# Windowed attention laid out by even and odd heads on the query partitions, with attention times values on eight array tiles

## The chip, the cores and the metric

One core of a Trainium2 chip, everything in fp32. The metric is the time of one execution on the device, in microseconds, median over several runs. The kernel before takes 4977.4 us (median of 3 runs, 4976.43 to 4993.0). PE is the matrix engine (TensorE), DVE the vector, ACT the scalar and POOL the GpSimd engine. A "row" is one row of eight 7x7 windows of one image; there are 32 images x 8 = 256 rows.

## The reference, cut to what matters

```python
# x: (32, 56, 56, 128); window 7x7 (49 tokens), 4 heads of 32 channels, shift by 3
def window_attention(x):                       # layer 0, after a group norm
    xs  = roll(x, (-3, -3)); win = windows(xs) # (B*64, 49, 128)
    q, k, v = split(win @ w_qkv.T)             # (.., 4 heads, 49, 32)
    attn = q * 32**-0.5 @ k.T + relative_bias + shift_mask
    out  = softmax(attn) @ v
    return roll(unwindow(out @ w_proj.T + b_proj), (3, 3))
x = x + window_attention(gn(x))
# layer 1: cosine transforms, mixing of 32 modes, back, and a feed-forward 128-512-128
x = x + feedforward(fourier(gn(x)))
```

The program runs the attention of one image together with layer 1 of the image before, so that PE has other work while attention waits for the other engines.

## The kernel before: the parts that the change and the argument touch

```python
# one row of windows, i; WT = 49, JP = 64, HD = 32, RT = 392
def attn_scores(im, i):
    pq = attn_bank()                               # query projection, copied by ACT into q
    nc.tensor.matmul(pq[:, :RT], lhsT=im.w[:, 0:C], rhs=src, ...)
    nc.scalar.activation(q[:, :RT], pq[:, :RT], AF.Identity, bias=im.bias[:, 0:1], scale=QS)
    pk = attn_bank()                               # key projection, then four fills of k_bd
    nc.tensor.matmul(pk[:, :RT], lhsT=im.w[:, C : 2 * C], rhs=src, ...)
    for h in range(NH):
        hs = slice(h * HD, (h + 1) * HD)
        dst = k_bd[hs, :, h % 2]                   # block diagonal: each head its own columns
        if h % 2:
            nc.vector.tensor_scalar(dst, pk3[hs], im.bias[hs, 1:2], None, ALU.add)
        else:
            nc.scalar.activation(dst, pk3[hs], AF.Identity, bias=im.bias[hs, 1:2])
    for w in range(NWR):                           # V, each window twice, by head parity hh
        for hh in range(2):
            nc.tensor.matmul(pv[hh * JP : hh * JP + WT, w * JP : (w + 1) * JP],
                             lhsT=src[:, w * WT : (w + 1) * WT], rhs=wv[:, hh], ...)
    # two ACT copies into v_bd; what lies off the head's own block stays zero
    for w in range(NWR):                           # scores: window parity on the partitions
        for hp in range(2):                        # hp: heads 0,1 or heads 2,3
            nc.tensor.matmul(
                ps[hp][(w % 2) * JP : (w % 2 + 1) * JP, (w // 2) * 2 * WT : (w // 2 + 1) * 2 * WT],
                lhsT=q[cs, w * WT : w * WT + JP],
                rhs=k_bd[cs, w].rearrange("c h j -> c (h j)"), ...)   # moves 98 columns
    # ... softmax on DVE, POOL, ACT ...

def attn_out(im, i):
    for hf in range(2):
        # 4 transposes into a bank, one DVE copy into aT, then per window (the last is cut in two)
        nc.tensor.matmul(po3[hp * JP : (hp + 1) * JP, :, x0 : x0 + s1 - s0],
                         lhsT=v[:, w, hp].rearrange("j h d -> j (h d)"),   # 128 x 64, half zeros
                         rhs=aT[:, 2 * (w4 // 2) + hp, w % 2, 0:WT]..., ...)
    nc.scalar.activation(oT[...], po[:, :RT], AF.Identity, bias=im.bias[:, 2:3])
    # ... projection by wproj, residual, store ...
```

## Time and profile before

| | kernel before |
|---|---|
| median time, first 3 runs | 4977.4 us |
| PE busy | 4641.3 us, 93% |
| DVE, ACT, POOL busy | 2428.6, 2491.8, 1385.5 us |
| one row, inner part | 18.88 us |

How to read the rest: PE's busy share says that it is the bound, but not how long each matmul holds it, since their records overlap. For that I use the start times of single records. A *group* is a run of matmuls of the same tiles (so the two projections L286 and L291 are one group where they adjoin); its *in-group time* goes from its first start to its last; its *switch* goes from its last start to the first start of the next group, less any wait; *idle* is what the profile calls a wait of PE. In-group, switch and idle add up to a row's length. I count from the start of row 40 to that of row 232 of each trace and divide by these 192 rows.

### The profile page before, as it was taken

Reading aid. Unit: us, or ns where it says so; the run is one execution under the profiler, and the core shown is the slowest. Engines: PE = TensorE matmul, PEld = TensorE weight load, DVE = VectorE, ACT = ScalarE, POOL = GpSimd, SP = SyncE. Lnnn points to the kernel's source line nnn. Section 1 sums busy time; section 2 is a strip of 40 time slices with the busy share of each in tenths; the row PEclk is TensorE's granted clock in tenths of the full one; section 3 lists DMA queues with packets and bytes.
Section 4 is the critical chain, followed back from the end, with each engine's and each line's share of the span. In section 5 each row is a group of like instructions: output and inputs, shape, how many; then the busy total and the mean of one; then the engine's idle time right before and its main releaser. Section 6 shows DMA issues by size and latency. Waiting matters only on the chain.

```text
span 4980.0 us, 143896 instructions
## 1 busy us (share of the span) xinstructions
PE 4641.3 (93%) x64320; PEld 3587.0 (72%) x64320; DVE 2428.6 (49%) x4469; ACT 2491.8 (50%) x4705; POOL 1385.5 (28%) x1071
## 2 busy tenths in 40 slices
PE   4799999999999999999999999999999999999998
PEld 3677777777777777777777777777777777777776
DVE  3554445554554545445544455544455544555441
ACT  2445555555555455554555555455554555554553
POOL 2222222232222323222232222222223232222220
PEclk8799999999999999999999999999999999999999
DMA  3111222212222212222212222122222122222111
GB/s 79 39 51 43 60 58 57 65 45 49 58 58 59 65 38 52 60 58 59 58 38 60 57 56 65 45 49 57 57 61 64 41 50 60 58 61 60 35 46 51
DMA packets 533292, 271.74 MB, mean 55 GB/s; under 512 B 29360, under 2 KB 532289, under 8 KB 532417
## 3 DMA queue, kind: packets, MB, share of 16 engines
q1 hardware_dynamic: 521272, 257.03, 20.3%
q8 instruction: 504, 8.26, 0.7%
q10 hardware_dynamic: 11400, 5.51, 0.4%
q14 instruction: 116, 0.94, 0.1%
HBM read 159.66 MB, written 102.76 MB: 53 GB/s over the span
## 4 chain that ended last, share of the span: by engine, by line
PE 72%; DVE 10%; ACT 7%; POOL 5%; issue 3%; DMA 2%; ACTq 1%; SPq 0%; POOLq 0%; DVEq 0%
PE pc L619 14%; PE pc L602 11%; PE pa L324 6%; PE pa L379 6%; PE pc L526 5%; PE pa L304 5%; POOL a L346 5%; PE pa L400 5%; PE pc L555 5%; PE pa L286 4%; PE pa L291 3%; DVE mx L345 3%; PE pa L365 2%; ACT a L349 2%; PE pa L230 2%
## 5 line engine op out<-in xcount | busy, mean ns | idle before, releaser
L619 PE MATMUL pc<-wff,hid 128*112 128x128 f32 x7168 | 926.5, 283 | 0.7 <-ACT hid L610 0.6
L619 PEld LDWEIGHTS pc<-wff,hid 128*112 128x112 f32 x7168 | 840.8, 182 | 55.1 <-issue 14.6
L346 POOL TENSOR_TENSOR a<-a,mx 128x784 f32<-128x784 f32 x256 | 389.0, 1519 | 1700.2 <-DVE mx L345 1586.2
L610 ACT ACTIVATE hid<-pc,b1sb 128x448 f32<-128x448 f32 x896 | 568.3, 634 | 487.4 <-PE pc L602 446.9
L602 PE MATMUL pc<-xf,wff 128*128 128x448 f32 x1792 | 781.1, 553 | 0.8 <-DVE xf L582 0.8
L349 ACT ACTIVATE a<-a 128x784 f32<-128x784 f32 x256 | 223.5, 873 | 835.5 <-POOL a L346 835.5
L297 DVE TENSOR_SCALAR k_bd<-pa,bqkv 32x392 f32<-32x392 f32 x512 | 320.7, 626 | 619.8 <-ACT k_bd L299 613.7
L352 POOL TENSOR_TENSOR a<-a,rs 128x784 f32<-128x784 f32 x256 | 389.1, 1520 | 678.1 <-DVE rs L351 595.8
L596 POOL TENSOR_TENSOR res<-res,b2sb 112x512 f32<-112x512 f32 x224 | 284.8, 1271 | 859.2 <-DMA res<-scr 837.5
L337 DVE TENSOR_TENSOR a<-pa,bm 128x392 f32<-128x392 f32 x512 | 284.8, 567 | 408.2 <-PE pa L324 403.5
L379 PEld LDWEIGHTS pa<-aT,v 128*64 128x64 f32 x9216 | 328.9, 142 | 166.4 <-DVE aT L371 121.1
L371 DVE COPY aT<-pa 128x512 f32<-128x512 f32 x512 | 346.1, 676 | 200.2 <-PE pa L365 199.9
L408 DVE TENSOR_TENSOR xl<-pa,xl 112x384 f32<-112x384 f32 (+1 forms) x256 | 159.9, 625 | 579.6 <-PE pa L400 579.6
L350 DVE TENSOR_REDUCE sm<-a 128x16 f32<-128x784 f32 x256 | 248.3, 970 | 387.5 <-ACT a L349 387.5
L324 PE MATMUL pa<-k_bd,q 64*64 64x98 f32 x8192 | 420.8, 252 | 16.6 <-DVE k_bd L297 13.7
L324 PEld LDWEIGHTS pa<-k_bd,q 64*64 64x64 f32 x8192 | 327.4, 133 | 143.4 <-DVE k_bd L297 85.3
L379 PE MATMUL pa<-aT,v 128*64 128x49 f32 (+2 forms) x9216 | 386.8, 227 | 35.7 <-DVE aT L371 33.5
L602 PEld LDWEIGHTS pc<-xf,wff 128*128 128x128 f32 x1792 | 300.4, 190 | 164.5 <-issue 91.8
L304 PEld LDWEIGHTS pa<-wn,xw 128*49 128x49 f32 x8192 | 258.8, 125 | 161.6 <-issue 63.4
L242 POOL TENSOR_TENSOR xl<-xl,bproj 112x384 f32<-112x384 f32 (+1 forms) x256 | 285.2, 1136 | 237.8 <-PE pa L230 234.3
L365 PE MATMUL pa<-ident,a 128*128 128x128 f32 x2048 | 334.8, 287 | 1.1 <-POOL a L352 1.1
L313 ACT COPY v<-pa 49x512 f32<-49x512 f32 x512 | 293.3, 573 | 78.0 <-PE pa L304 72.4
(83 smaller groups left out, 6687.3 us busy)
## 6 DMA issues: line engine op xcount, KB each, us to landing
res<-scr SPq DMA_DIRECT2D x224, 224.0 KB
htok<-scr SPq DMA_DIRECT2D x256, 196.0 KB
out_dram<-res SPq DMA_DIRECT2D x192, 224.0 KB
scr<-xl SPq DMA_DIRECT2D x128, 224.0 KB
xl<-in_x_dram SPq DMA_DIRECT2D x32, 784.0 KB
xl<-in_x_dram SPq DMA_DIRECT2D x32, 672.0 KB
scr<-xl SPq DMA_DIRECT2D x128, 168.0 KB
out_dram<-res SPq DMA_DIRECT2D x32, 112.0 KB
```

The costliest lines, as they stand in the source:

```text
L297: nc.vector.tensor_scalar(dst, pk3[hs], im.bias[hs, 1:2], None, ALU.add)
L304: nc.tensor.matmul(pv[hh * JP : hh * JP + WT, w * JP : (w + 1) * JP], lhsT=src[:, w * WT : (w + 1) * WT], rhs=wv[:, hh], start=True, stop= ...
L324: nc.tensor.matmul(ps[hp][qs, (w // 2) * 2 * WT : (w // 2 + 1) * 2 * WT], lhsT=q[cs, w * WT : w * WT + JP], rhs=k_bd[cs, w].rearrange("c h ...
L346: nc.gpsimd.tensor_tensor(a3, a3, mx2.unsqueeze(2).to_broadcast([P, 2 * NR, WT]), ALU.subtract)
L349: nc.scalar.activation(a3, a3, AF.Exp)
L352: nc.gpsimd.tensor_tensor(a3, a3, rs2.unsqueeze(2).to_broadcast([P, 2 * NR, WT]), ALU.mult)
L365: nc.tensor.transpose(pt[:, m * P : (m + 1) * P], a[:, hp, pr].rearrange("p h j -> p (h j)"), ident,)
L371: nc.vector.tensor_copy(aT.rearrange("p m a j -> p (m a j)"), pt)
L379: nc.tensor.matmul(po3[hp * JP : (hp + 1) * JP, :, x0 : x0 + s1 - s0], lhsT=v[:, w, hp].rearrange("j h d -> j (h d)"), rhs=aT[:, 2 * (w4 / ...
L602: nc.tensor.matmul(ph[:, :GT], lhsT=wff1[:, f * P : (f + 1) * P], rhs=xf[:, 8 * g : 8 * g + 8].rearrange("p r w -> p (r w)"), start=True, ...
L610: nc.scalar.activation(hf, ph[:, :GT], AF.Relu, bias=b1sb[:, f : f + 1])
L619: nc.tensor.matmul(pf[:TC, c * C : (c + 1) * C], lhsT=hid[f][:, c * TC : (c + 1) * TC], rhs=wff2[:, f], start=(f == 0), stop=(f == NF - 1),)
```

## The change

The intent is that attention times values does not multiply the zeros of a block-diagonal V. The query partitions of a score tile now hold head parity (u) where they held window parity. So the transposed attention has, on its first 64 partitions, an even window, and on the others an odd one (in the kernel before an even and an odd head, which is why V had to be block-diagonal there). Values can take 49 rows and 32 columns for each window and head, on eight tiles of the array. V gets half as many matmuls, twice as wide, and one copy instead of two. The price lies in scores: each moves 49 columns instead of 98, and there are twice as many. Output comes in two banks, by parity of the window, and is brought into order by ACT (one piece) and DVE (three pieces).

```diff
         for w in range(NWR):
             for hp in range(2):
                 cs = slice(hp * JP, (hp + 1) * JP)
-                qs = slice((w % 2) * JP, (w % 2 + 1) * JP)
-                nc.tensor.matmul(
-                    ps[hp][qs, (w // 2) * 2 * WT : (w // 2 + 1) * 2 * WT],
-                    lhsT=q[cs, w * WT : w * WT + JP],
-                    rhs=k_bd[cs, w].rearrange("c h j -> c (h j)"),
...
+                for u in range(2):
+                    nc.tensor.matmul(
+                        ps[hp][u * JP : (u + 1) * JP, w * WT : (w + 1) * WT],
+                        lhsT=q[cs, w * WT : w * WT + JP],
+                        rhs=k_bd[cs, w, u],
...
         for w in range(NWR):
-            for hh in range(2):
-                nc.tensor.matmul(
-                    pv[hh * JP : hh * JP + WT, w * JP : (w + 1) * JP],
-                    lhsT=src[:, w * WT : (w + 1) * WT],
-                    rhs=wv[:, hh],
...
+            t0 = i * RT + w * WT
+            nc.tensor.matmul(
+                pv[w % 2 * JP : (w % 2 + 1) * JP, (w // 2) * C : (w // 2 + 1) * C],
+                lhsT=im.xw[:, t0 : t0 + JP],
+                rhs=im.w[:, 2 * C : 3 * C],
...
+        nc.scalar.copy(v.rearrange("j p c -> j (p c)"), pv)
...
-                    for hp in range(2):
                         nc.tensor.matmul(
-                            po3[hp * JP : (hp + 1) * JP, :, x0 : x0 + s1 - s0],
-                            lhsT=v[:, w, hp].rearrange("j h d -> j (h d)"),
...
+            for p2 in range(2):
+                pr = 2 * hf + p2
+                for h in range(NH):
+                    for u in range(2):
+                        ks = slice(u * JP, u * JP + WT)
+                        nc.tensor.matmul(
+                            po[u][h * HD : (h + 1) * HD, pr * WT : (pr + 1) * WT],
+                            lhsT=v[ks, pr, h * HD : (h + 1) * HD],
+                            rhs=aT[ks, 2 * p2 + h // 2, h % 2, 0:WT],
...
-        nc.scalar.activation(
-            oT[:, i % 2 * RT : (i % 2 + 1) * RT], po[:, :RT], AF.Identity, bias=im.bias[:, 2:3]
-        )
+        # for each bank u: the piece of u = 0 on ACT, the three of u = 1 on DVE
+                if u:
+                    nc.vector.tensor_scalar(d, f, im.bias[:, 2:3], None, ALU.add)
+                else:
+                    nc.scalar.activation(d, f, AF.Identity, bias=im.bias[:, 2:3])
```

Cut: the bias and mask tables in the new order, the buffers, and the address arithmetic of the output pieces (the comment line stands for it).

More of the change, by code (lines that the diff above doesn't have):

```diff
@@ L152, in swin_fourier_kernel @@
     nc.sync.dma_start(rpb[JP : JP + WT], rpb[0:WT])
-    mask_sb = const_load([P, 2, 3, WT], shift_mask.rearrange("r s p j -> p r s j"), "mask")
-    bm = const.tile([P, 2, 2, NWR // 2, 2, WT], F32, tag="bm", name="bm")
-    rpb_f = rpb.rearrange("p (t h) y x -> p t h (y x)", t=2)
-    for r in range(2):
-        for pr in range(NWR // 2):
-            for t in range(2):
-                nc.vector.tensor_tensor(
-                    bm[:, r, t, pr],
-                    rpb_f[:, t],
-                    mask_sb[:, r, 0 if pr < NWR // 2 - 1 else 2]
-                    .unsqueeze(1)
-                    .to_broadcast([P, 2, WT]),
-                    ALU.add,
-                )
+    mask_sb = const.tile([P, 2, 2, WT], F32, tag="mask", name="mask")
+    nc.vector.memset(mask_sb, 0.0)
+    for hh in range(2):
+        rows = slice(hh * JP, hh * JP + WT)
+        for k, src in enumerate((shift_mask[:, 0, 0:WT], shift_mask[:, 2, JP : JP + WT])):
+            nc.scalar.dma_start(mask_sb[rows, :, k], src.rearrange("r p j -> p r j"))
+    bm = const.tile([P, 2, 2, NWR, WT], F32, tag="bm", name="bm")
+    nc.gpsimd.memset(bm, 0.0)
+    rpb_f = rpb.rearrange("p (t u) y x -> p t u (y x)", u=2)
+    for r in range(2):
+        for t in range(2):
+            for u in range(2):
+                rows = slice(u * JP, u * JP + WT)
+                for k, w0_, w1_ in ((0, 0, NWR - 1), (1, NWR - 1, NWR)):
+                    n = w1_ - w0_
+                    nc.vector.tensor_tensor(
+                        bm[rows, r, t, w0_:w1_],
+                        rpb_f[rows, t, u].unsqueeze(1).to_broadcast([WT, n, WT]),
+                        mask_sb[rows, r, k].unsqueeze(1).to_broadcast([WT, n, WT]),
+                        ALU.add,
+                    )
     dct_w = const_load([TC, 2 * NM], dct, "dct_w")
@@ L197, in swin_fourier_kernel @@
     nc.gpsimd.memset(k_bd, 0.0)
-    q_sb, v_bd, a_sb = [], [], []
+    q_sb, v_sb, a_sb = [], [], []
     for i in range(2):
         q_sb.append(big.tile([P, RT + JP - WT], F32, tag=f"q{i}", name=f"q{i}"))
-        v_bd.append(big.tile([P, NWR, 2, 2, HD], F32, tag=f"v{i}", name=f"v{i}"))
-        a_sb.append(big.tile([P, 2, NWR // 2, 2, JP], F32, tag=f"a{i}", name=f"a{i}"))
+        v_sb.append(big.tile([P, NWR // 2, C], F32, tag=f"v{i}", name=f"v{i}"))
+        a_sb.append(big.tile([P, 2, NWR, JP], F32, tag=f"a{i}", name=f"a{i}"))
         nc.gpsimd.memset(q_sb[i], 0.0)
-        nc.gpsimd.memset(v_bd[i], 0.0)
         nc.gpsimd.memset(a_sb[i], 0.0)
@@ L216, in image_begin @@
         im.x = xls.pop(b) if b in xls else load_image(b)
-        im.xw = big.tile([P, NWR, RT], F32, tag="xw", name="xw", bufs=2)
+        im.xw = big.tile([P, NWR * RT + JP - WT], F32, tag="xw", name="xw", bufs=2)
+        nc.gpsimd.memset(im.xw[:, NWR * RT :], 0.0)
         im.st = small.tile([P, NWR, 6], F32, tag="st0", name="st0", bufs=2)
@@ L235, in image_group @@
         mine = pt4[:, :, i % 2 : i % 2 + WS].rearrange("p j r s -> p j (r s)")
-        xw = im.xw[:, i]
+        xw = im.xw[:, i * RT : (i + 1) * RT]
         nc.scalar.copy(xw.rearrange("p (j t) -> p j t", t=WT), mine)
@@ L281, in attn_scores @@
     def attn_scores(im, i):
-        q, v, a = q_sb[i % 2], v_bd[i % 2], a_sb[i % 2]
-        src = im.xw[:, i]
+        q, v, a = q_sb[i % 2], v_sb[i % 2], a_sb[i % 2]
+        src = im.xw[:, i * RT : (i + 1) * RT]
         pq = attn_bank()
@@ L300, in attn_scores @@
         pv = attn_bank()
-        wv = im.w[:, 2 * C : 3 * C].rearrange("c (p h d) -> c h p d", h=2, d=HD)
         for w in range(NWR):
-            for hh in range(2):
-                nc.tensor.matmul(
-                    pv[hh * JP : hh * JP + WT, w * JP : (w + 1) * JP],
-                    lhsT=src[:, w * WT : (w + 1) * WT],
-                    rhs=wv[:, hh],
-                    start=True,
-                    stop=True,
-                )
-        for hh in range(2):
-            rows = slice(hh * JP, hh * JP + WT)
-            nc.scalar.copy(
-                v[rows, :, :, hh].rearrange("j w p d -> j (w p) d"),
-                pv[rows].rearrange("j (x d) -> j x d", d=HD),
+            t0 = i * RT + w * WT
[3 more added lines that the diff above has]
+                rhs=im.w[:, 2 * C : 3 * C],
+                start=True,
+                stop=True,
             )
+        nc.scalar.copy(v.rearrange("j p c -> j (p c)"), pv)
         ps = [attn_bank(), attn_bank()]
@@ L322, in attn_scores @@
                 cs = slice(hp * JP, (hp + 1) * JP)
-                qs = slice((w % 2) * JP, (w % 2 + 1) * JP)
-                nc.tensor.matmul(
-                    ps[hp][qs, (w // 2) * 2 * WT : (w // 2 + 1) * 2 * WT],
-                    lhsT=q[cs, w * WT : w * WT + JP],
-                    rhs=k_bd[cs, w].rearrange("c h j -> c (h j)"),
-                    start=True,
-                    stop=True,
-                )
-        NR = NWR // 2 * 2
+                for u in range(2):
[3 more added lines that the diff above has]
+                        rhs=k_bd[cs, w, u],
+                        start=True,
+                        stop=True,
+                    )
+        NR = NWR
         mx = small.tile([P, 2, NR], F32, tag="mx", name="mx")
@@ L335, in attn_scores @@
         for hp in range(2):
-            a3 = a[:, hp].rearrange("p a h j -> p (a h) j")[:, :, 0:WT]
+            a3 = a[:, hp, :, 0:WT]
             nc.vector.tensor_tensor(
@@ L339, in attn_scores @@
                 ps[hp][:, :RT].rearrange("p (m j) -> p m j", j=WT),
-                bm[:, i // (NWR - 1), hp].rearrange("p a h j -> p (a h) j"),
+                bm[:, i // (NWR - 1), hp],
                 ALU.add,
             )
-        a3 = a.rearrange("p t a h j -> p (t a h) j")[:, :, 0:WT]
+        a3 = a.rearrange("p t w j -> p (t w) j")[:, :, 0:WT]
         mx2, sm2, rs2 = (t.rearrange("p t m -> p (t m)") for t in (mx, sm, rs))
@@ L356, in attn_out @@
     def attn_out(im, i):
-        v, a = v_bd[i % 2], a_sb[i % 2]
-        po = attn_bank()
-        po3 = po[:, :RT].rearrange("p (r x) -> p r x", x=S)
+        v, a = v_sb[i % 2], a_sb[i % 2]
+        po = [attn_bank(), attn_bank()]
+        HALF = RT // 2
         for hf in range(2):
@@ L366, in attn_out @@
                     pt[:, m * P : (m + 1) * P],
-                    a[:, hp, pr].rearrange("p h j -> p (h j)"),
+                    a[:, hp, 2 * pr : 2 * pr + 2].rearrange("p w j -> p (w j)"),
                     ident,
@@ L371, in attn_out @@
             nc.vector.tensor_copy(aT.rearrange("p m a j -> p (m a j)"), pt)
-            for w4 in range(4):
-                w = 4 * hf + w4
-                x0 = w * WS + SS
-                cuts = ((0, WS, x0),) if w < NWR - 1 else ((0, WS - SS, x0), (WS - SS, WS, 0))
-                for s0, s1, x0 in cuts:
-                    for hp in range(2):
-                        nc.tensor.matmul(
-                            po3[hp * JP : (hp + 1) * JP, :, x0 : x0 + s1 - s0],
-                            lhsT=v[:, w, hp].rearrange("j h d -> j (h d)"),
-                            rhs=aT[:, 2 * (w4 // 2) + hp, w % 2, 0:WT].rearrange(
-                                "j (r s) -> j r s", s=WS
-                            )[:, :, s0:s1],
+            for p2 in range(2):
+                pr = 2 * hf + p2
+                for h in range(NH):
+                    for u in range(2):
+                        ks = slice(u * JP, u * JP + WT)
+                        nc.tensor.matmul(
+                            po[u][h * HD : (h + 1) * HD, pr * WT : (pr + 1) * WT],
+                            lhsT=v[ks, pr, h * HD : (h + 1) * HD],
+                            rhs=aT[ks, 2 * p2 + h // 2, h % 2, 0:WT],
                             start=True,
@@ L391, in attn_out @@
         oT = im.oT
-        nc.scalar.activation(
-            oT[:, i % 2 * RT : (i % 2 + 1) * RT], po[:, :RT], AF.Identity, bias=im.bias[:, 2:3]
-        )
+        oTr = oT[:, i % 2 * RT : (i % 2 + 1) * RT].rearrange("p (r x) -> p r x", x=S)
+        for u in range(2):
+            src = po[u][:, :HALF].rearrange("p (j r s) -> p j r s", r=WS, s=WS)
+            n = NWR // 2 - u
+            x0 = SS + u * WS
+            dst = oTr[:, :, x0 : x0 + (n - 1) * 2 * WS + WS]
+            parts = [
+                (bass.AP(dst.tensor, dst.offset, [dst.ap[0], [2 * WS, n], [S, WS], [1, WS]]), src[:, :n])
+            ]
+            if u:
+                parts.append((oTr[:, :, S - WS + SS : S], src[:, n, :, : WS - SS]))
+                parts.append((oTr[:, :, 0:SS], src[:, n, :, WS - SS :]))
+            for d, f in parts:
+                if u:
+                    nc.vector.tensor_scalar(d, f, im.bias[:, 2:3], None, ALU.add)
+                else:
+                    nc.scalar.activation(d, f, AF.Identity, bias=im.bias[:, 2:3])
         n0, n1 = WS * i // 2, WS * (i + 1) // 2
```

## The prediction

> **What bounds the kernel now.** I read the page first, busy times and slices, then the table by stretches, the groups, what the matrix engine waited for, and the timeline of one row of windows. From the page:
>
> ```profile
> PE 4641.3 (93%) x64320; PEld 3587.0 (72%) x64320; DVE 2428.6 (49%) x4469; ACT 2491.8 (50%) x4705; POOL 1385.5 (28%) x1071
> PE   4799999999999999999999999999999999999998
> DMA  3111222212222212222212222122222122222111
> ```
>
> PE is busy in every slice but the first three; the vector and scalar engines stand at half, DMA at a fifth. The table by stretches, for one inner millisecond:
>
> ```profile
> 1500.00:2500.00 1000.00, 951.74 (x13261) 738.12 (x13259) 500.43 (x921) 510.19 (x957) 283.52 (x217) 0.98 0.22 57
> ```
>
> So PE is idle 5% of the inner part (columns: stretch, length, then PE, weight load, DVE, ACT, POOL busy, clock, DMA). The view of what PE waited for has its two attention entries small:
>
> ```profile
> PE pc L555 <- ACT zT L550: 119.2, 138, 1.5
> PE pa L379 <- DVE aT L371: 33.5, 92, 0.8
> PE pa L400 <- ACT oT L392: 19.9, 40, 1.2
> ```
>
> Even with every attention wait gone, 1% is to be had. The kernel is bound by PE's in-order stream: attention of one image, with the Fourier layer of the image before as filler. There are 32 x 8 = 256 rows of windows, and the inner part passes some 19 us per row. What counts is **how long PE is held per row**, not latency. The groups that the change touches, then the timeline of one row and of another where scores ran as one block:
>
> ```profile
> L324 PE MATMUL pa<-k_bd,q 64*64 64x98 f32 x8192 | 420.8, 252 | 16.6 <-DVE k_bd L297 13.7
> L379 PE MATMUL pa<-aT,v 128*64 128x49 f32 (+2 forms) x9216 | 386.8, 227 | 35.7 <-DVE aT L371 33.5
> L304 PE MATMUL pa<-wn,xw 128*49 128x64 f32 x8192 | 310.4, 223 | 0.0
> L313 ACT COPY v<-pa 49x512 f32<-49x512 f32 x512 | 293.3, 573 | 78.0 <-PE pa L304 72.4
> ```
>
> ```profile
> 2563.43 1.10 PE L304 MATMUL pa<-wn,xw 128*49 128x64 f32 x32
> 2564.46 1.02 PE L602 MATMUL pc<-xf,wff 128*128 128x448 f32 x2
> ...
> 2565.41 0.89 PE L324 MATMUL pa<-k_bd,q 64*64 64x98 f32 x16
> 2566.23 1.02 PE L602 MATMUL pc<-xf,wff 128*128 128x448 f32 x2
> ...
> 2567.18 0.89 PE L324 MATMUL pa<-k_bd,q 64*64 64x98 f32 x16
> 2568.00 1.77 PE L602 MATMUL pc<-xf,wff 128*128 128x448 f32 x4
> ...
> 2571.22 0.67 PE L379 MATMUL pa<-aT,v 128*64 128x49 f32 x16
> ...
> 2573.91 0.77 PE L379 MATMUL pa<-aT,v 128*64 128x49 f32 x20
> ```
>
> ```profile
> 2504.62 1.05 PE L324 MATMUL pa<-k_bd,q 64*64 64x98 f32 x32
> ```
>
> Every fp32 matmul of the source is two in the trace. The mean of 227 to 252 ns is latency and misleads: they overlap. PE is held from a group's start to the start of the next: V 2563.43 to 2564.46 is 1.03 us; scores 0.82 + 0.82 = 1.64 us in two halves; attention times values 0.60 + 0.70 = 1.30 us (next groups at 2571.82 and 2574.61). Scores come in halves because the key tile of heads 0 and 1 is ready 1.2 us before that of heads 2 and 3 (ACT and DVE fill it in four steps of about 0.6 us). Counting the single records after 500 us, 172 of 230 rows have the halves apart; in the rest all four tiles of the array take part, and 32 matmuls cost 0.81 us from first to last start, where a half of 16 costs 0.65 us.
>
> The starts of single records give the law. Neighbouring matmuls on different tiles start 6 to 7 ns apart; the same tile is ready again after a period: 56 ns (V, 49 weight columns, 64 moving), 58 to 59 ns (values, 64 weight, 49 moving), 84 ns (scores, 64 and 98), 96 ns (L555, 64 and 112). All fit max(weight columns, moving columns) / 1.2 per ns plus 3 to 6 ns. A start in a new tiling costs about 0.05 us more at the first gap, and from the last start to the next group there pass 0.15 to 0.2 us.
>
> **What the Trainium skill says.** (1) "TensorE: Matmul & The Clock Gate", section "LDWEIGHTS (loading the stationary operand)": the time goes with the columns of the weights, columns / 1.2 ns, whatever the contraction. The trace agrees: 64 columns give 53 ns, and the L379 period is 58, though it moves only 49. (2) Same page, "Part 3: Packing small matmuls — row/col tiling": matmuls on different tiles run concurrently, about 4 ns apart in start. The trace has 6 to 7 ns. (3) Same page, "Wait — 56ns, not 53.3ns?": start to start never drops below about 25 ns however small N. Between tiles this trace contradicts it (7 ns, at most four in a row); whether it comes back as a mean over eight tiles no run here shows yet. (4) "TensorEngine Tiling (Array Packing)", "Key Properties": changing the tiling mode drains the engine; the 0.15 to 0.2 us above are that size.
>
> **The change, part by part, per row.**
> V: 32 matmuls of 64 moving columns become 16 of 128, weights 64. Period 128/1.2 + 3 = 110 ns for two column tiles: 8 x 110 = 0.88 us, now 0.88 us (32 records). **0 us.** The two ACT copies (573 ns each) become one of 128x512, some 0.6 us: ACT -0.55 us.
>
> Scores: 32 matmuls moving 98 become 64 moving 49, so the same query weights are loaded for both head parities. The period falls only from 84 to 58 ns, as the weight load of 64 columns now bounds it, and there are twice as many. A half: 16 periods x 58 = 0.93, plus 0.05 at the start and 0.17 to the next group, 1.15 us against 0.82. In two halves +0.66 us. As one block on four tiles: 16 periods x 58 = 0.93 + 0.22 = 1.15 against 0.98, +0.17 us. Weighted 75 to 25: **+0.54 us.**
>
> Values: 36 matmuls on two tiles (weights 128x64, half zeros) become 64 on eight (49 rows, 32 weight columns, 49 moving). A tile's period is 49/1.2 + 3 = 44 ns, shorter than eight starts of 7 ns. So a half row is 32 x 7 = 0.22 + 0.05 + 0.17 = 0.44 us, the row 0.88 against 1.30: **-0.42 us** at best. If issue can't hold 7 ns over 32 in a row and gives some 15 (my assumption, no row shows it), a half takes 32 x 8 = 0.26 us more, the row 0.51 us, and the saving turns into +0.09 us. I take -0.25 us, a little nearer to the full rate than to that, as the middle.
>
> Output: one ACT evacuation of 587 ns becomes ACT on 196 columns, some 0.33 us (from 587 for 392 and 369 for 224), and DVE on 147 + 28 + 21 columns, some 0.33 + 0.19 + 0.18 = 0.7 us (from 626 for 392 and 158 for 1). ACT -0.25, DVE +0.7. These engines go to about 46 and 52%; they lie beside PE.
>
> Softmax, transposes, projection and transfers keep their sizes. Values now hold two of the four attention banks from the first half to the evacuation, with one or two more for the transposes; PE has the Fourier work as filler, so I give this 0 to 0.1 us. Start: three more DMA issues on ACT, whose queue is what the first copy waits for (until 49.8 us), 2 us in all. Lighter ACT may shorten the 119 us of waits for zT by some 20 us.
>
> Sum: +0.54 - 0.25 = +0.29 us a row; x 256 = +74 us; + 2 + 13 (banks, 0.05 a row) - 20 = +69 us: **5046 us, 1.4% slower.**
>
> **Rivals.** A: eight tiles at full rate and scores mostly as one block: +0.17 - 0.42 = -0.25 us, x 256 = -64 us, with the ACT relief about 4890 us. For it: the schedule is made anew and twice as many matmuls may let the second half become ready while the first runs. Against: the key tile is still filled in the same four steps. B: issue becomes the bound. A row has 16 + 64 + 64 = 144 matmuls where it had 32 + 32 + 36 = 100. At 15 to 20 ns each the 64 of values cost 0.96 to 1.28 us, plus 0.44 for two starts and ends, 1.40 to 1.72 against 1.30; with the scores +0.64 to +0.96 us a row, 5140 to 5225 us. For it: point (3); against: bursts of 7 ns. C: a new wait on the banks or on DVE's three small evacuations ahead of the projection (0.7 us where ACT took 0.59), shown by L400 waiting longer: +0.2 us a row if the filler doesn't cover it, +50 us. D: ACT relief dominates: the ACT waits of PE in the Fourier part are below 200 us in all, so even half of it is 2%.
>
> **Range and chances.** Best combination 4890, middle 5046, issue-bound 5140 and more. Range 4910 to 5190. The middle lies 31 us under the 2% mark (5077), and B and C lie above it, A within 2% below: slower 0.35, same 0.59, faster 0.06.
>
> **What would show it.** Scores: 16384 records, nominally, of 64x49, period 58 to 59 ns on the same tile, PE held about 1.15 us for a half; if the period is below 50, the weight-load step is wrong. Values: 16384 records 64*32, a half of 32 from first to last start in about 0.3 us; 0.5 or more means issue is the bound (B). V: 4096 records at 55 ns in the mean. ACT busy about 2290 us, DVE about 2610 us. L400's waits near the 20 us of now, or C. The prediction is wrong if the halves of scores merge, or if the seven-nanosecond starts do not hold.

## More of the kernel before

```profile
core 0: 4980.0 us, clock 0.977
```

That is the line of the core: its span and the mean clock that PE was granted. The records of the clock list stretches at 1.00 and at 0.50, nothing between, so 0.977 means some 4 to 5% of the time at half.

## The result, and the profile after

The changed kernel is correct and takes 5067.91 us (median of 4 runs, 5059.22 to 5071.16); the kernel before took 4980.56 us in the same rounds. Ratios here are the mean time of one kernel's fast runs over that of the other's fast runs of the same rounds, so not quite the ratio of the medians that are quoted. The ratio is 1.0168, with a 95% interval of 1.0146 to 1.0191: slower, by less than 2%.

The page after, busy times and the slices of PE:

```profile
PE 4683.1 (92%) x75584; PEld 3592.8 (71%) x75584; DVE 2589.6 (51%) x5238; ACT 2307.7 (46%) x4449; POOL 1388.7 (27%) x1102
PE   4799999999999999999999999999999999999998
```

The same millisecond as before, in the table by stretches, and then the groups of the three attention steps and the V copy:

```profile
1500.00:2500.00 1000.00, 945.11 (x15151) 724.75 (x15151) 524.33 (x1065) 464.14 (x891) 285.70 (x226) 0.98 0.20 53
```

```profile
L329 PE MATMUL pa<-k_bd,q 64*64 64x49 f32 x16384 | 594.6, 221 | 2.8 <-DVE k_bd L305 1.5 <-ACT k_bd L307 0.2
...
L384 PE MATMUL pa<-aT,v 49*32 49x49 f32 x16384 | 238.5, 214 | 106.6 <-DVE aT L378 101.9 <-issue 4.7
...
L320 ACT COPY v<-pa 128x512 f32<-128x512 f32 x256 | 151.1, 590 | 75.5 <-PE pa L313 69.4
```

PE is still the bound. Scores grew from 420.8 to 594.6 us of busy time, values fell from 386.8 to 238.5, while the mean of one record only went from 252 and 227 ns to 221 and 214: it is mostly latency, and does not say how long PE is held. What changed beside the sizes is the idle time before values, 106.6 us where it was 35.7. The view of what PE waited for:

```profile
PE pc L574 <- ACT zT L569: 108.2, 201, 1.2
PE pa L384 <- DVE aT L378: 101.9, 164, 1.3
PE pa L419 <- DVE oT L411: 46.5, 37, 3.0
```

The wait for zT is a little shorter, that for aT three times as long, and the projection's wait has gone from 19.9 us for ACT to 46.5 for DVE. Now the timeline of one row:

```profile
1580.29 1.13 PE L329 MATMUL pa<-k_bd,q 64*64 64x49 f32 x32
1581.35 0.47 PE L638 MATMUL pc<-wff,hid 128*112 128x128 f32 x2
1581.75 1.13 PE L329 MATMUL pa<-k_bd,q 64*64 64x49 f32 x30
...
1586.36 0.40 PE L384 MATMUL pa<-aT,v 49*32 49x49 f32 x32
...
1588.98 0.41 PE L384 MATMUL pa<-aT,v 49*32 49x49 f32 x32 [0.67 <-DVE aT L378]
```

A half of scores holds PE 1.06 us (1580.29 to 1581.35) where it held 0.82; a half of values 0.33 us (to 1586.69, the next group) where it held 0.60 to 0.70. The second half of values waits 0.67 us for the copy of the transposed attention. The single records, in us per row:

| per row, rows 40 to 232 | before | after | difference |
|---|---|---|---|
| in-group: scores | 1.133 | 1.667 | +0.53 |
| in-group: values | 1.027 | 0.438 | -0.59 |
| in-group: V | 0.904 | 0.860 | -0.04 |
| in-group: all else, the same matmuls | 10.69 | 10.86 | +0.18 |
| switches (21.67 and 23.12 groups) | 4.20 | 4.34 | +0.14 |
| idle | 0.92 | 1.08 | +0.16 |
| **row** | **18.88** | **19.26** | **+0.38** |

0.38 x 256 = 97 us, against 87 measured in all. Three lines were asked for by the change (scores, values, V) and come to -0.10 us; the other three outweigh them. The switches have a plain source: scores come in 3.62 groups a row, not 2.38. Part of a switch is the last matmul's own time, its moving columns over 1.2 per ns. Beyond that, the next group starts 96 ns later where it uses tiles of another size, and 2 ns later where it does not (medians of 2,172 and 1,639 switches of the trace before, without a wait and at full clock). Such changes of size number 13.1 a row before and 15.3 after, which makes some 0.2 us by this estimate.

The odd line is "all else": matmuls that nobody touched take longer (+0.14 if one groups by source line). Most of that goes with the clock, which is at half for 140 us against 92 in these rows: half of the difference is 0.12 us a row. The same 32 matmuls of one line, twice in the timeline after, 155 us apart; the waits ahead of them are the same:

```profile
1603.06 1.92 PE L545 MATMUL pc<-y,w1sb 128*64 128x56 f32 x32 [0.85 <-ACT y L512]
```

```profile
1758.48 1.15 PE L545 MATMUL pc<-y,w1sb 128*64 128x56 f32 x32 [0.85 <-ACT y L512]
```

And the stretches around the first, with the clock in the third column from the right:

```profile
1595.00:1603.00 8.00, 6.42 (x174) 5.63 (x170) 3.98 (x7) 4.23 (x7) 1.52 (x1) 1.00 0.98 230
1603.50:1606.80 3.30, 3.30 (x54) 2.75 (x52) 0.94 (x3) 0.53 (x1) 2.58 (x2) 0.51 0.09 25
1607.00:1615.00 8.00, 8.00 (x165) 6.36 (x162) 3.74 (x9) 4.62 (x11) 0.00 (x0) 1.00 0.11 31
```

From 1603.3 us on PE is busy all the time and at half clock for 3.4 us. Why? The records of the clock change only at multiples of 3.41 us, so I cut all twelve traces into such windows (inner part, without some 0.3 ms at each end; windows at full clock: 15,075) and asked which property of a window foretells that the next one is at half clock. What separates best of what I tried is an *array share*: for each matmul, rows x columns x moved columns, over 128 x 128, over 1.2 per ns, summed and divided by the window. In the window ahead of the one shown it was 0.28, and PE was busy for 52% of it.

| array share of the window | windows | next window at half clock |
|---|---|---|
| under 0.34 | 286 | 226 |
| 0.34 to 0.38 | 413 | 52 |
| 0.38 to 0.45 | 742 | 2 |
| over 0.45 | 13,634 | 0 |

PE's busy share alone separates them less well: among all the windows, its best single limit leaves 194 on the wrong side, that of the array share 114. Of 1,674 windows with PE busy 50 to 80%, 164 of 224 with a share under 0.34 fell, 52 of 394 between 0.34 and 0.38, and 2 of 1,056 above. Waits belong to it all the same: no window with PE busy over 80% was followed by half clock (0 of some 13,350), and nearly all under 50% were (62 of 65).

The zeros that the kernel before multiplied counted as work in this sum. The change takes them away, and the mean share falls from 0.676 to 0.652. The mean tells little, however: experiment 1 takes no zeros away, has 0.655 because its rows are longer, and is at half clock for 99 us. Nor does the change have many more falls than the kernel before, 25 stretches at half clock against 24 in these rows. They last longer, 1.64 windows against 1.12. For how long one lasts, the array share and the waits of PE foretell about equally well (best single limits 37 and 24 wrong of 395 half-clock windows), so the traces alone do not tell the two apart there. So far this is a correlation; experiments 4, 5 and 8 try it.

### The profile page after: what moved, and what is told of

Same layout as the page of the kernel before. It is cut to its first block, busy times and chain, and to the rows that moved or that the text cites. A ratio compares the mean times of both kernels' runs of the same rounds, so it can differ in the third digit from the quotient of the medians.

```text
span 5066.5 us, 167329 instructions
## 1 busy us (share of the span) xinstructions
PE 4683.1 (92%) x75584; PEld 3592.8 (71%) x75584; DVE 2589.6 (51%) x5238; ACT 2307.7 (46%) x4449; POOL 1388.7 (27%) x1102
## 5 line engine op out<-in xcount | busy, mean ns | idle before, releaser
L638 PE MATMUL pc<-wff,hid 128*112 128x128 f32 x7168 | 901.9, 278 | 0.1
L638 PEld LDWEIGHTS pc<-wff,hid 128*112 128x112 f32 x7168 | 813.2, 177 | 56.4 <-issue 17.1
L621 PE MATMUL pc<-xf,wff 128*128 128x448 f32 x1792 | 768.7, 552 | 0.8 <-DVE xf L601 0.8
L329 PEld LDWEIGHTS pa<-k_bd,q 64*64 64x64 f32 x16384 | 511.6, 134 | 141.3 <-issue 84.3
L329 PE MATMUL pa<-k_bd,q 64*64 64x49 f32 x16384 | 594.6, 221 | 2.8 <-DVE k_bd L305 1.5
L384 PEld LDWEIGHTS pa<-aT,v 49*32 49x32 f32 x16384 | 153.4, 108 | 267.1 <-DVE aT L378 217.5
L384 PE MATMUL pa<-aT,v 49*32 49x49 f32 x16384 | 238.5, 214 | 106.6 <-DVE aT L378 101.9
L313 PEld LDWEIGHTS pa<-wn,xw 128*64 128x64 f32 x4096 | 231.2, 137 | 144.0 <-issue 60.9
L307 ACT ACTIVATE k_bd<-pa,bqkv 32x392 f32<-32x392 f32 x512 | 297.7, 581 | 66.0 <-DVE k_bd L305 41.7
```

Of the source, the lines that this page charges most:

```text
L329: nc.tensor.matmul(ps[hp][u * JP : (u + 1) * JP, w * WT : (w + 1) * WT], lhsT=q[cs, w * WT : w * WT + JP], rhs=k_bd[cs, w, u], start=True, ...
L384: nc.tensor.matmul(po[u][h * HD : (h + 1) * HD, pr * WT : (pr + 1) * WT], lhsT=v[ks, pr, h * HD : (h + 1) * HD], rhs=aT[ks, 2 * p2 + h // ...
L621: nc.tensor.matmul(ph[:, :GT], lhsT=wff1[:, f * P : (f + 1) * P], rhs=xf[:, 8 * g : 8 * g + 8].rearrange("p r w -> p (r w)"), start=True, ...
L638: nc.tensor.matmul(pf[:TC, c * C : (c + 1) * C], lhsT=hid[f][:, c * TC : (c + 1) * TC], rhs=wff2[:, f], start=(f == 0), stop=(f == NF - 1),)
```

## The experiments

The theory: scores cost what I predicted (1); in how many groups they come is worth more than the change itself (2, 3); values save time on PE, but a part of it is lost to the half clock, because the array does less (4, 5, 8). The rivals: the layout loses for a reason that neither clock nor groups cover (2 against 3); or the new output pieces on DVE make the new waits (7). The clock's part took its form with the traces of the first four runs; 5 and 8 were made to test it. Each run has one short edit. Experiments 1 to 4 ran on one chip, 5 to 8 on a second, 9 and 10 on a third, each time beside runs of the kernel before; so compare ratios.

### 1. The kernel before, each score matmul split in two

```diff
-                    rhs=k_bd[cs, w].rearrange("c h j -> c (h j)"),      # 98 columns
+                for h in range(2):
...
+                            ps[hp][qs, (2 * pr + h) * WT : (2 * pr + h + 1) * WT],
+                            rhs=k_bd[cs, w, h],                         # 49 columns, twice
```

> The kernel before, with only its scores done as in the change: each 64x98 matmul is two of 64x49 with the query weights loaded twice, still two column tiles in turn; values, V and evacuations are as before. Theory (the doubled scores cost what the values on eight tiles save): in-group time of the scores goes from 1.13 us a row to about 1.67, as in the changed kernel, and the whole to about 5110 us, +2.6% (between +1.8 and +3.3%). Rival (the doubled scores are hidden or cheap, and the loss of the change lies in its waits for aT, its throttled clock and DVE's evacuations): under +1%, 5030 us or less.

Measured: 5112.11 us, ratio 1.0247 (1.0211 to 1.0283). In-group scores 1.532 us a row, under the 1.67 that I expected. Groups view, timeline and the longest wait:

```profile
L326 PE MATMUL pa<-k_bd,q 64*64 64x49 f32 x16384 | 555.6, 222 | 2.2 <-ACT k_bd L299 1.2 <-DVE k_bd L297 0.4
```

```profile
2506.38 1.06 PE L326 MATMUL pa<-k_bd,q 64*64 64x49 f32 x32
```

```profile
PE pa L381 <- DVE aT L373: 105.8, 140, 1.3
```

The price of the doubled scores, with what their schedule brings, is 2.5%, close to the 2.6% that I expected. Half the columns per matmul saves little (58 ns a period for 84), for the weights still have 64 columns. One more thing is seen here: values in the old form wait 105.8 us for aT, not 33.5. So the longer wait for aT comes with the schedule around the doubled scores, and does not need the values' new form.

### 2 and 3. Scores as one block, in the changed kernel and in the kernel before

One ordering edge per row: the first score matmul waits for the last of the four key fills, so that all scores run together on four tiles instead of two halves on two.

```diff
-                nc.vector.tensor_scalar(dst, pk3[hs], im.bias[hs, 1:2], None, ALU.add)
+                last_k = nc.vector.tensor_scalar(dst, pk3[hs], im.bias[hs, 1:2], None, ALU.add)
...
-                    nc.tensor.matmul(
+                    mm = nc.tensor.matmul(
...
+                    if w == 0 and hp == 0 and u == 0:
+                        tc.add_manual_dep(mm.ins, last_k.ins.name, DEP, reason="one block")
```

(Experiment 3 has the same edge, without u.)

> The changed kernel, with one ordering edge a row: the first score matmul waits for the last of the four key fills, so that all 64 run as one block on four tiles (before the chip, the program order shows 254 of 256 rows as one block). Theory: PE is held by scores for some 1.17 us a row instead of 2.06, so about -0.85 us a row, 4850 us; at least 130 us below the changed kernel, thus faster than the kernel before by 1 to 3%. Rival (waits for aT, clock, DVE bind): less than 40 us gained on the changed kernel, above 5025 us, since PE then only waits elsewhere.

> The kernel before with the same edge: its 32 score matmuls run as one block on four tiles in all 256 rows. Theory: held time from 1.71 to about 1.0 us a row where the halves were apart; some -0.5 us a row, 4860 us, -2.4%. With both orders repaired, the layout of the change should be no slower than the old one: e2 over e3 between 0.985 and 1.010. Rival: the layout itself loses (waits, clock): e2 stays 1.5% or more above e3.

Measured: the change with one block 4936.85 us, ratio to before 0.9902 (0.9870 to 0.9933), 87 us short of the gain that I expected, and just the 130 us below the change that I had named as the least; the kernel before with one block 4842.21 us, ratio 0.9708 (0.9684 to 0.9732). Timeline of the two blocks, changed kernel, then kernel before:

```profile
1589.73 1.15 PE L330 MATMUL pa<-k_bd,q 64*64 64x49 f32 x64
1590.81 0.33 PE L566 MATMUL pc<-ident,z 128*128 128x128 f32 x1
```

```profile
1599.38 0.91 PE L325 MATMUL pa<-k_bd,q 64*64 64x98 f32 x32 [1.59 <-DVE k_bd L298]
```

64 matmuls in 1.08 us where two halves took 2.12; per row in-group scores fall from 1.667 to 0.935, and from 1.133 to 0.661 in the old layout. That is 2.6% and 2.9%, more than the whole change moved the time. It isn't free: the view of waits shows what is paid back, changed kernel first:

```profile
PE pc L577 <- ACT zT L572: 188.3, 256, 1.4
```

```profile
PE pa L325 <- DVE k_bd L298: 126.3, 98, 3.9
```

In its own right the pair is a miss for my theory. With the groups alike, I expected the two layouts within 0.985 to 1.010 of each other; the ratio is 1.020. The rival "the layout loses" stands, and what it consists of had to be found. The mean granted clock over all their executions is 0.966 against 0.9805: that can be 1.5% at most. In the two traces a row takes 18.64 us against 18.32. Scores cost 0.27 us more, values and V 0.64 less, so in the groups that it touches the layout wins. It loses in idle time, +0.25 us (zT 0.74 against 0.25, the key fills 0.12 against 0.49, over all 256 rows), and in switches and all else, +0.44, of which some 0.17 is half clock (130 us against 65). Why the waits for zT grow isn't shown.

### 4 and 5. Values on four tiles, with and without the zeros

In the kernel before, the values alone: per head, 32 weight columns, on four tiles; experiment 4 takes 49 rows (no zeros), experiment 5 all 128 (with the zeros, on four columns of tiles). Same count of matmuls, same 32 columns.

```diff
+                        for h in range(2):
+                            ks = slice(h * JP, h * JP + WT)
-                            lhsT=v[:, w, hp].rearrange("j h d -> j (h d)"),
+                            lhsT=v[ks, w, hp, h],        # 4: 49 rows;  5: v[:, w, hp, h], 128 rows
+                            rhs=aT[ks, ...]              # 4: 49 rows;  5: aT[:, ...]
```

> The kernel before, with values without zeros in the old layout: each 128x64 matmul becomes two of 49 rows by 32 columns (one per head), on four tiles (row tile tied to column tile), 72 matmuls in the trace for 36; scores untouched. Theory: period 44 ns for four tiles, 11 ns each, in-group 0.8 us a row for 1.03: -0.2 us a row, 4930 us, -1%. If values were not on the path, or the zeros cost nothing: 0 +- 0.4%.

> As e4 in number, order and length of the values' matmuls (72 in the trace a row, 49 moving, 32 weight columns, four tiles), but each contracts over all 128 rows, zeros included, so only the share of the array that works differs: 128 rows for 49. In the single records of six traces so far, a 3.4 us window in which rows x columns x moving columns come to under some 0.35 of the full array is what precedes a fall of the clock to half; above 0.38 none does. Theory (the zeros kept the clock up): same in-group time as e4 (0.78 us a row), half-clock time in rows 40 to 232 back from 150 us to about 92 us as before, and 4930 us, -1.2% against before, 1.6% under e4. Rival (e4 lost its gain to waits, and the clock is chance): as e4, +0.5%, half-clock time 130 us or more.

Measured: 5011.81 us, ratio 1.0046 (1.0014 to 1.0078), and 4976.6 us, ratio 0.9986 (0.9968 to 1.0004). Line of the core and timeline, experiment 4, then 5:

```profile
core 0: 5026.2 us, clock 0.964
```

```profile
2021.58 0.58 PE L381 MATMUL pa<-aT,v 49*32 49x49 f32 x40
```

```profile
core 0: 4975.3 us, clock 0.975
```

```profile
2020.65 0.58 PE L380 MATMUL pa<-aT,v 128*32 128x49 f32 x40 [0.53 <-DVE aT L371]
```

To PE's stream the two are the same: 40 matmuls in 0.58 us, in-group 0.784 and 0.764 us a row where the kernel before has 1.027. Yet the one without zeros is *slower* than the kernel before, by 0.5%, and the one with zeros is not. The order of the matmul records, by the names of their tiles, is the same in both traces, all 73,536 of them, and the waits are nearly alike (138.0 and 139.8 us for zT, 49.9 and 49.0 for aT). The profiled executions differ at 0.964 and 0.975, but that of experiment 4 was its slowest; over all executions the mean clock is 0.9708 and 0.9783 (the kernel before beside them: 0.9743 and 0.9756). The array share is 0.648 and 0.676. In rows 40 to 232 the half clock lasts 150 us in experiment 4 and 68 in experiment 5: half of the difference is 0.21 us a row, and the rows differ by 0.20 (19.05 and 18.85). This was the test of the clock: give the zeros back, change nothing else, and the half clock goes back. It did: mean clock 0.75% higher, time 0.6% shorter, 35 us between the medians of two chips (the kernel before differs by 9 us between them). One rival is left here: with 128 rows the tiles have another shape. Experiment 8 keeps the shape. Over the 25 executions of the kernel before, too, time goes against the mean clock (correlation -0.82).

The gain in time that I had expected was missed both times (-1% and -1.2%). A saving of 0.26 x 256 = 67 us in group shows as 7 in experiment 5, which is not clear of zero. I can name part of where it went: idle time is +0.17 us a row, 44 us; the wait for zT rose from 119.2 to 139.8 us in all and that for aT from 33.5 to 49.0. PE gets to the end of values sooner and then waits for the other engines.

### 6. The kernel before with one block and with values on four columns

This adds the edits of 3 and 5.

> e3 (scores in one block on four tiles) with the values of e5. Theory: the gains add, 4842 - 55 = 4790 us, -4.1% against before. Rival: with the scores in one block the values' time is filled by waits for aT, no further gain: 4840 us.

Measured: 4809.04 us, between the theory's 4790 and the rival's 4840; ratio 0.9647 (0.9629 to 0.9664), mean clock 0.9838. With the block in place the same values are worth 0.6%, not 0.1%. What is left in the view of waits is the block's own price:

```profile
PE pa L325 <- DVE k_bd L298: 126.6, 102, 3.2
```

### 7. The changed kernel, all output pieces on ACT

```diff
-                if u:
-                    nc.vector.tensor_scalar(d, f, im.bias[:, 2:3], None, ALU.add)
-                else:
-                    nc.scalar.activation(d, f, AF.Identity, bias=im.bias[:, 2:3])
+                nc.scalar.activation(d, f, AF.Identity, bias=im.bias[:, 2:3])
```

> The changed kernel, with all four output evacuations on ACT and none on DVE. Theory: PE's waits for oT in front of the projection (46 us from DVE) and some of those for aT fall, DVE goes from 2590 to about 2415 us busy; 20 to 50 us gained on the changed kernel, 5020 to 5050 us. Rival (DVE is not what is waited for): within 0.3% of the changed kernel, 5055 to 5085 us.

Measured: 5086.77 us, ratio 1.0199 (1.0176 to 1.0222), not clear of the change's 1.0168, since the intervals overlap, and just above the range of the rival by which DVE isn't the cause. The gain that I expected isn't there. The waits:

```profile
PE pa L384 <- DVE aT L378: 102.2, 163, 1.3
PE pc L571 <- ACT zT L566: 88.7, 171, 1.2
PE pa L416 <- ACT oT L410: 84.2, 95, 2.6
```

DVE does 161 us less, and the wait for aT, which DVE makes, is what it was (101.9). So a crowded DVE does not make that wait. The wait before the projection has only moved to ACT, and grew to 84.2 us. Moving the pieces gained nothing.

### 8. The changed kernel, one block, values over 64 rows

Experiment 2 with 15 rows of zeros added to each values matmul: the test of the clock from the other side, in the new layout.

```diff
-                        ks = slice(u * JP, u * JP + WT)
+                        ks = slice(u * JP, (u + 1) * JP)
```

> e2 with the values' matmuls over 64 rows for 49 (15 rows of zeros added, same time on PE by the columns): the array works 31% more in the values. Theory of the clock: half-clock time falls a little, from 130 us to some 110 in rows 40 to 232, 0 to 0.4% under e2 (4917 to 4937 us). Rival: no difference.

Measured: 4908.06 us, ratio 0.9848 (0.9827 to 0.9869), against 0.9902 of experiment 2. Multiplying more zeros is 0.5% faster; mean clock 0.9725 against 0.966, the order of all 75,584 matmul records is the same, and the waits are alike (190.5 us for zT, 94.7 for aT; in experiment 2, 188.3 and 95.0). In rows 40 to 232 the half clock goes from 130 us to 89, which is 0.11 us a row, and the row from 18.64 to 18.55. So more zeros mean less half clock in both layouts, here without a change of tile shape. The two ran on two chips, each beside the kernel before. The gain is larger than the upper end that I gave.

### 9 and 10. Key projection first, in both layouts

The block waits for the key fills, so these should start as soon as they can. The key projection and its fills are put ahead of the query projection and its copy: experiment 9 on top of 6, experiment 10 on top of 8.

```diff
-        pq = attn_bank()
-        nc.tensor.matmul(pq[:, :RT], lhsT=im.w[:, 0:C], rhs=src, start=True, stop=True)
-        nc.scalar.activation(q[:, :RT], pq[:, :RT], ...)
         pk = attn_bank()
...
+        pq = attn_bank()
+        nc.tensor.matmul(pq[:, :RT], lhsT=im.w[:, 0:C], rhs=src, start=True, stop=True)
+        nc.scalar.activation(q[:, :RT], pq[:, :RT], ...)
```

> e6 with the key projection and its four fills ahead of the query projection and its copy. In e6 PE waits 0.45 us a row for the key tile, in front of the one block of scores. Theory: the last fill comes about 0.6 us earlier (ACT no longer copies the query first), so most of that wait goes: -0.2 to -0.4 us a row, 4710 to 4760 us. Rival: the query's copy is then last, or another wait takes its place, 4780 us or more.

> e8 (the change's layout, scores in one block, values over 64 rows) with the same key-first order. There PE waits only 0.05 us a row for the key tile, since its order has Fourier work in front of it. Theory: little, within 0.8% of e8, 4870 to 4945 us, and so the old layout with the same repairs stays ahead by 2% or more. Rival: the new layout catches up, under 4840 us.

Measured: 4771.99 us, ratio 0.9581 (0.9566 to 0.9595), and 4928.2 us, ratio 0.9897. In experiment 9 the wait for the key fills falls from 126.6 to 69.0 us:

```profile
PE pa L325 <- DVE k_bd L293: 69.0, 100, 3.9
```

It is the best version, 4.2% faster than the kernel before, and faster than the changed kernel; it missed the range that I gave it by a little. The changed kernel with the same repairs doesn't gain from this step (0.9897, 0.9879 to 0.9915, against 0.9848 on another chip), as expected, and stays 3% behind.

## Why the prediction was right or wrong, point by point

The time was 22 us above the one predicted, inside the range, and the class (within 2%) was the likeliest. The single steps did less well than the sum, so part of this is luck.

- **Scores, +0.54 us a row: right.** In-group +0.53; 32 records span 911 ns from first to last start: 15 periods of 58 to 59 ns, the second tile's offset and some 20 to 30 ns more at the start; experiment 1 has its price alone. Not foreseen was that the halves would be cut further: 3.62 groups a row for 2.38. With that the switches of all kinds grew by 0.14 us. Point (4) of the prediction laid the whole 0.15 to 0.2 us before the next group to the change of tiling; it is 0.10, and the rest is the last matmul's own time.
- **Values, -0.25 us: mis-sized, -0.59 in group.** I had put it halfway because issue might not hold 7 ns over eight tiles. It does: 32 records span 201 ns (median of 372 groups), 6.5 ns each, and the gain is more than my best case of 0.42. A wait for aT, which went from 0.09 to 0.38 us a row, took half of it back, so the -0.30 left lies near my -0.25 by luck. That wait came with the doubled scores, as experiment 1 shows. Why the schedule around them makes it isn't shown; experiment 7 rules out that DVE is too full.
- **V, 0 us: right** (-0.04). V copy 590 ns, as reckoned (0.6 us).
- **ACT and DVE: right**, 2307.7 and 2589.6 us for some 2290 and 2610. They lie beside PE.
- **Rival C, the wait before the projection: seen, but small**: 19.9 to 47.4 us (46.5 for DVE, 0.9 for ACT). That is +28 us where I had put 13 into the sum for the banks. Moving the pieces to ACT gained nothing.
- **zT, -20 us for a lighter ACT:** -11. **Start, +2:** the first wait is 41.6 to 43.3 us.
- **Rival B, issue as the bound: wrong.** Point (3) of the prediction asked for the 25 ns as a mean over eight tiles; it is 6.5.
- **Missing altogether: the clock.** The prediction took the duration of unchanged matmuls as given. They took 0.18 us a row more, 46 us in 256 rows, most of it from half-clock windows (140 us for 92: half the difference of 48 us, over the 192 rows, is 0.12 us a row). I had the mean clock on the page and did not ask what makes it.

So the sum came out right by luck, since two errors met: values were worth more than I took, and the switches, the wait for aT and the clock cost what I had not taken.

What stays open: why the schedules differ as they do, for the order of instructions on PE is made anew for each program and one edit moves many groups; the last 0.5% or so between experiments 2 and 3, which the clock can't explain; and what exact quantity the clock follows, for the array share is the best of those I tried and still leaves 114 of the 15,075 windows on the wrong side of the best single limit. Nor is it shown what part waits have in it.

## What to carry to other kernels

Price a packed matmul by the larger of its weight columns and its moving columns (the periods of 56 to 96 ns in these traces fit that), then look at how many groups the scheduler makes of it: joining two halves into one block was worth 2.6 to 2.9% here, more than taking the zeros out of values. When matmuls are made smaller, look at the granted clock of both kernels: work saved on the array, even work on zeros, can be given back by a slower clock, and the test is to put the zeros back and see. A faster step in the middle of a chain only helps as far as the engines around it deliver in time, so read the idle time before the *next* step, too.

## What the Trainium skill lacked or had wrong

- "TensorE: Matmul & The Clock Gate", section "Wait — 56ns, not 53.3ns?": start to start is said never to drop below about 25 ns. Between different tiles it does: 32 matmuls on eight tiles start 6.5 ns apart in the mean (201 ns from first to last). The sentence lacks the exception that the page's own "Part 3: Packing small matmuls — row/col tiling" makes with 4 ns or so, which is somewhat less than measured here.
- Same page, "Part 1: The HAM clock gate (the "warmup" mystery)": the gate is said to go by how busy PE has been, and after an idle window to fall to half. The two states and the window of 3.41 us agree with the traces. But windows with PE busy 50 to 80% fell or did not according to the array share (rows x columns x moved columns): 164 of 224 under 0.34, 2 of 1,056 over 0.38. None of some 13,350 windows busy over 80% fell. Products with zeros count as work (experiments 5 and 8: 68 us at half clock for 150, 89 for 130); the page does not say what a small matmul counts for.
- Same page, "Part 4: PE-mode transpose": a transpose is said not to count as PE-busy in the same way. In these traces, for fp32, it seems to count in full: with transposes in the array share the best single limit leaves 114 of 15,075 windows on the wrong side, with half their weight 176, and without them 263. That is a fit and no experiment, and the records don't say whether these transposes ran in the mode that the page means.
- "TensorEngine Tiling (Array Packing)", "Key Properties": a change of tiling mode drains the engine, without a figure. In the trace before, the first start after a change of tile size comes 96 ns later than the last matmul's moving columns account for, and 2 ns where the size stays (medians of 2,172 and 1,639).
